# A scaled copy moved to VectorE, activation tables visited together, and a norm's scale and bias folded into weights, in a selective-scan and MLP kernel

## The chip, the cores and the metric

The kernel runs on one core of a Trainium2 chip. A core has five engines that work side by side, each through its own queue in order: TensorE (PE, with its weight loads as PEld), VectorE (DVE), ScalarE (ACT), GpSimd (POOL) and SyncE (SP), which issues most DMAs. Times are microseconds on the device. The median of three runs counts.

## The reference, cut to what matters

The input x has four images of 256 x 64 positions with 128 channels. Layer 0 turns each image into 64 sequences of 256 tokens, runs a selective scan over each in both directions, and adds an MLP:

```python
h = layernorm(xs, g1, b1)
xc, z = split(h @ W_in.T)                       # 2 x 256 channels
# for each direction:
u  = silu(causal_conv(xc))                      # 256 channels, 4 taps
xdbl = u @ Wx_.T                                # 8 + 16 + 16
dt = softplus(xdbl[..., :8] @ Wdt_.T + bdt_)
h_t = exp(dt_t * A) * h_{t-1} + (dt_t * u_t) * B_t   # 16 states a channel
y_t = sum_n h_t[n] * C_t[n];  y = (y + u * D) * silu(z)
# both directions added:
y  = layernorm((y_f + y_b) @ W_out.T, g2, b2)
xo = y + xs
h2 = layernorm(xo, g3, b3)
out = xo + gelu(h2 @ W1m + b1m) @ W2m + b2m
```

A group norm over the whole image stands ahead of layer 0 and of layer 1. Layer 1 projects each position, convolves two 16-channel maps with 3 x 7 kernels and mixes them with products per position ("mixing" below).

## The kernel before

An image is cut into 32 groups of two sequences (512 tokens, `COLS`); with four images there are 128 groups, `G` = 0 to 127. A group has 32 units, one for each direction `i` and state `n`. The main loop runs over the 4096 units `k`, and around each unit it steps generators that hold the rest of the work, one yield or so a step.

For a unit:

- `inputs(k + 3)` makes `dbt`, the product of `duT` (dt times u, tokens on partitions) with one column of B, as four copies of 128x256 scaled by a column, on ScalarE (L472); and `decay`, two exponentials on ScalarE (L478), behind a small GpSimd memset (L476).
- `turned` transposes `dbt` into the PSUM banks `db` on TensorE (L492).
- `scanned` runs two scans on VectorE (L504), one for each half of the channels, with `decay` from SBUF and `db` from PSUM.
- `weighted` multiplies the states by C on GpSimd (L510), in SBUF.
- `added` adds them up over n in PSUM on TensorE (L532); a group's first `added` puts the D term in first (L519).

`dbt`, `decay` and `hs` have four buffers each. The scaled copies run three units ahead of the scans (`AHEAD`), the additions two behind (`LAG`).

For a group, `front(G)` prepares it: load, first norm, convolution on TensorE (L359), silu, the projections (L378, L408), softplus (L307), du on GpSimd (L418), its transposes (L431), then z. It starts `LEAD` units ahead of the group's first one. While it prepares u and dt it is stepped twice a unit. PSUM results are moved out by `evacuated`: on VectorE in the first image (`G < NGRP`, L301 and L303), on ScalarE later (L299). `back(G)` finishes a group: copies of y (L549), gating with z (L561), the output projection, second norm, residual (L571, L574), third norm (L578, L582, L586), MLP up (L591, L593), gelu (L313), MLP down and residual (L615), statistics and store.

`inverse_std` gives a norm's factor: Square on ScalarE (L275), a mean by matmul (L278), then Ln and Exp on ScalarE (L281, L283). A `lock` lets one norm at a time through. Three PSUM banks (`take`, `give`) are shared by fronts, backs, statistics and layer 1; a step that needs one waits until one is free.

ScalarE holds one activation table at a time. Exp and Ln share one, to which `both_tables` (L204) returns after each visit to another: silu (L289, L291), softplus (L307), gelu (L313). `softplus` also runs the gelu of any back that stands in `waiting`; a back that was not taken along within three steps runs its own. Within an engine, the framework orders instructions by program order and its own estimate of when each is ready; `keep_in_program_order` pins an instruction behind all that was written before it on its engine.

In the first image layer 1 has no work yet. From the second on, `project` and `mix` run beside the scans, with large VectorE products and sums (L755, L840, L851, L766); when all units are done, `mix_alone` does the rest.

Of the kernel before, what the change touches and what calls it, by code (L numbers as in the profile page):

```python
# [13 lines left out]
F32 = mybir.dt.float32  # L14
AF = mybir.ActivationFunctionType
ALU = mybir.AluOpType
AX = mybir.AxisListType
PSUM = bass.MemoryType.PSUM
# [14 lines left out]
COLS = 512  # L33
# [6 lines left out]
def fused_kernel(ctx: ExitStack, tc: tile.TileContext, a: dict, out: bass.AP):  # L40
    nc = tc.nc
    x = a["x"]
    B, T, N, _ = x.shape
    SG = COLS // T
    NGRP = N // SG
    TH = T // 128
    RB = 128 // N
    CB = COLS // 128
# [4 lines left out]
    KVT = (T + 2) * N  # L53
    AHEAD, LAG = 3, 2
    UNITS = 2 * NS
    LEAD = 50


    const = ctx.enter_context(tc.tile_pool(name="const", bufs=1))
# [14 lines left out]
    centre = const.tile([128, 128], F32, name="centre")  # L74
# [17 lines left out]
    g1, b1, g2, b2, g3, b3 = (column(f"L0_conv_{k}") for k in ("g1", "b1", "g2", "b2", "g3", "b3"))  # L92
    b1m, b2m = column("L0_conv_b1m"), column("L0_conv_b2m")
# [6 lines left out]
    w1m = load("w1m", [128, FF], a["L0_conv_W1m"])  # L100
# [25 lines left out]
    nc.vector.tensor_scalar(w_om, w_om, 1.0 / C, None, ALU.mult)  # L126
    for h in range(2):
        nc.vector.tensor_scalar(w_out[:, h, :], w_out[:, h, :], w_om[:, h, :], None, ALU.subtract)


    w_cv, neg_a, diag_d = [], [], []
# [30 lines left out]
    p1 = ctx.enter_context(tc.tile_pool(name="p1", bufs=1))  # L162
# [36 lines left out]
    def later(turns):  # L199
        for _ in range(turns):  # L200
            yield 1, 0
# [65 lines left out]
    waiting = []  # L267
    pending = []

    def inverse_std(centred):  # L270
        while lock:
            yield 1, 0
        lock.append(1)
        sq = p1.tile([128, COLS], F32, name="sq")
        nc.scalar.activation(sq, centred, AF.Square)  # L275
        yield 1, 1
        var = take()
        nc.tensor.matmul(var, lhsT=mean_c, rhs=sq, start=True, stop=True)  # L278
        yield 1, 0
        rstd = p1.tile([128, COLS], F32, name="rstd")  # L280
        nc.scalar.activation(rstd, var, AF.Ln, bias=eps_ln)  # L281
        give(var)
        nc.scalar.activation(rstd, rstd, AF.Exp, scale=-0.5)  # L283
        yield from later(2)
        return rstd

    def silu(*ts):
# [15 lines left out]
            nc.vector.tensor_scalar(to, bank, bias, None, ALU.add)  # L303

    def softplus(*ts):
        for dt in ts:
            nc.scalar.activation(dt, dt, AF.Softplus)  # L307
        gelu()
        both_tables()

# [6 lines left out]
    def front(G):  # L317
# [15 lines left out]
        xg = st["xg"] = p3.tile([128, COLS], F32, name="xg")  # L333
# [6 lines left out]
        rstd = yield from inverse_std(xc)  # L340
# [13 lines left out]
        for q in range(4):  # L354
            i, h = divmod(q, 2)
            cv = take()
            for k in range(KC):
# [3 lines left out]
                    lhsT=w_cv[i][:, k, h * 128 : (h + 1) * 128],  # L361
                    rhs=hp[:, :, o : o + T],
                    start=k == 0,
                    stop=k == KC - 1,
# [27 lines left out]
        bT = st["bT"] = p2.tile([128, 2, CB, NS], F32, name="bT")  # L392
# [12 lines left out]
        for q in range(4):  # L405
            i, h = divmod(q, 2)
            v = take()
            nc.tensor.matmul(v, lhsT=w_dt[i][:, h * 128 : (h + 1) * 128], rhs=xds[i], start=True, stop=True)  # L408
            yield 1, 0
            evacuated(G, dts[i][:, h, :], v, bdt[i][:, h : h + 1])  # L410
            give(v)
            yield (0, 1) if q < 3 else (1, 0)
        softplus(*dts)
        yield from later(2)
        for i in range(2):
# [8 lines left out]
            duT = st["duT", i] = p2.tile([128, CB, DI], F32, name="duT")  # L424
# [19 lines left out]
        for h in range(2):  # L444
# [3 lines left out]
                lhsT=w_z[:, h * 128 : (h + 1) * 128],  # L448
                rhs=h_in,
                start=True,  # L450
                stop=True,
# [14 lines left out]
    def inputs(G, i, n):  # L466

        st = state[G]
        dt, bT, duT = st["dt", i], st["bT"], st["duT", i]
        dbt = st["dbt", i, n] = p4.tile([128, CB, DI], F32, name="dbt")  # L470
        for j in range(CB):
            nc.scalar.mul(dbt[:, j, :], duT[:, j, :], bT[:, i, j, n : n + 1])  # L472
        da = st["da", i, n] = p4.tile([128, 2 * SG, T], F32, name="decay")
        lo = 1 - i

        nc.gpsimd.memset(da[:, :, (T - 1) * i : (T - 1) * i + 1], 0.0)  # L476
        for h in range(2):
            nc.scalar.activation(  # L478
                da[:, h * SG : (h + 1) * SG, lo : lo + T - 1],
                dt[:, h, :].rearrange("d (s t) -> d s t", s=SG)[:, :, lo : lo + T - 1],  # L480
                AF.Exp,
                scale=neg_a[i][:, h, n : n + 1],
            )
        if n == NS - 1:
            st[("half", "read")[i]] = True
# [56 lines left out]
    def back(G):  # L542

        b, g = divmod(G, NGRP)
        st = state[G]
        xg, sz = st["xg"], st["s"]
        yt = p1.tile([128, CB, 2, 128], F32, name="yt")
        for k in range(2):
            nc.scalar.copy(yt[:, 2 * k : 2 * k + 2], y[k])  # L549
        while (G > 0 and not state[G - 1].get("back")) or "silu" not in st:  # L550
            yield 1, 0
        xin = p1.tile([128, TH, SG, C], F32, name="xin2")
        nc.sync.dma_start(out=xin, in_=x_cols(b, g))
        yield 1, 1
        yz = p1.tile([128, 2, COLS], F32, name="yz", tag="wide")
        for h in range(2):
            yc = take()
            for j in range(CB):
                nc.tensor.transpose(yc[:, 128 * j : 128 * (j + 1)], yt[:, j, h, :], ident)
            yield 1, 0  # L560
            nc.vector.tensor_tensor(yz[:, h, :], yc, sz[:, h, :], ALU.mult)  # L561
            give(yc)
            yield (0, 1) if h == 0 else (1, 1)
        st["gated"] = True
        oc = take()
        for h in range(2):
            nc.tensor.matmul(oc, lhsT=w_out[:, h, :], rhs=yz[:, h, :], start=h == 0, stop=h == 1)
        yield 1, 0
        rstd = yield from inverse_std(oc)
        xo = p1.tile([128, COLS], F32, name="xo")  # L570
        nc.vector.scalar_tensor_tensor(xo, oc, g2, rstd, ALU.mult, ALU.mult)  # L571
        lock.pop()
        give(oc)
        nc.vector.scalar_tensor_tensor(xo, xo, b2, xg, ALU.add, ALU.add)  # L574
        st["joined"] = True
        yield 1, 1
        xc3 = take()
        nc.tensor.matmul(xc3, lhsT=centre, rhs=xo, start=True, stop=True)  # L578
        yield 1, 0
        rstd = yield from inverse_std(xc3)  # L580
        h3 = p1.tile([128, COLS], F32, name="h3")
        nc.vector.scalar_tensor_tensor(h3, xc3, g3, rstd, ALU.mult, ALU.mult)  # L582
        lock.pop()
        give(xc3)
        yield 1, 0
        nc.scalar.activation(h3, h3, AF.Identity, bias=b3)  # L586
        yield 1, 1
        ge = p1.tile([128, 2, COLS], F32, name="ge", tag="wide")
        for h in range(2):
            m1 = take()  # L590
            nc.tensor.matmul(m1, lhsT=w1m[:, h * 128 : (h + 1) * 128], rhs=h3, start=True, stop=True)  # L591
            yield 1, 0
            nc.vector.tensor_scalar(ge[:, h, :], m1, b1m[:, h : h + 1], None, ALU.add)  # L593
            give(m1)
            yield (0, 1) if h == 0 else (1, 0)
        st["ge"] = ge
        waiting.append(st)
        for _ in range(3):
            if "gelu" not in st:
                yield 1, 0  # L600
        if "gelu" not in st:
            gelu()
            both_tables()
        yield from later(2)
        yield 1, 1

        m2 = take()
        for h in range(2):
            nc.tensor.matmul(
                m2, lhsT=w2m[:, h, :], rhs=ge[:, h, :], start=h == 0, stop=False, skip_group_check=True  # L610
            )
        turned_x(m2, xin, add=True)
        yield 1, 0
        x1 = p1.tile([128, COLS], F32, name="x1")
        nc.vector.scalar_tensor_tensor(x1, m2, b2m, xo, ALU.add, ALU.add)  # L615
        give(m2)
        yield 1, 1
        nc.vector.bn_stats(im[b]["stats2"][:, g, :], x1)
        op = take()
        for j in range(CB):  # L620
            nc.tensor.transpose(op[:, 128 * j : 128 * (j + 1)], x1[:, 128 * j : 128 * (j + 1)], ident)
        yield 1, 0
        ot = p1.tile([128, SG, TH, C], F32, name="ot")
        nc.scalar.copy(ot.rearrange("t s h c -> t (s h c)"), op)
        give(op)
        yield 1, 0
        for h in range(TH):
            nc.sync.dma_start(
                out=im[b]["x1d"][128 * h : 128 * (h + 1), g * SG : (g + 1) * SG, :], in_=ot[:, :, h, :]
            )  # L630
        st["back"] = True
        if g == NGRP - 1:
            yield 1, 0
            yield from group_norm(im[b]["stats2"], im[b]["gn2"])
# [358 lines left out]
    for k in range(len(units) + LAG):  # L993
        G, at = divmod(k, UNITS)
# [119 lines left out]
```

## Time and profile before

| | us |
|---|---|
| median of 3 runs | 19500.96 (19493.19 to 19508.58) |
| profiled execution | 19461.56 (span 19459.8) |
| busy PE, PEld | 16942.8 (87%), 13087.9 (67%) |
| busy DVE | 16298.0 (84%) |
| busy ACT | 16155.3 (83%) |
| busy POOL | 11335.3 (58%) |

The costliest groups of the page are the GpSimd multiply L510 (4096 of 2375 ns), the scans L504 (8192 of 1203 ns), the scaled copies L472 (16384 of 499 ns, overlapping by some 75 ns) and the exponentials L478 (8192 of 711 ns). There are 995 table loads of 1283 ns: 420 at L204, 195 at L307, 128 each at L289 and L313, 124 elsewhere. Busy shares over the whole span mix stages that differ, so the stages are to be read apart.

### The profile page before, as it was taken

The numbers are of one execution on the slowest core, as the hardware profiler recorded it, in microseconds if no ns is written. First come the engines' busy times: TensorE is split into PE (matmuls) and PEld (weight loads), VectorE is DVE, ScalarE is ACT, GpSimd is POOL, SyncE is SP. The second block draws the span as 40 slices with busy tenths as digits, with TensorE's granted clock in tenths as the row PEclk, the third lists the DMA queues.
The fourth block names the chain that finished last, engine by engine and source line by source line (L and its number), as shares of the span: only waits on it lengthen the run. The fifth ranks groups of instructions, "written<-read, shape, count | busy, mean of one in ns | idle before, by whom it ended". The sixth has DMA issues, their size and how long they took to land. (4 is left out here: it accounts for less than half of the span.)

```text
span 19459.8 us, 310011 instructions
## 1 busy us (share of the span) xinstructions
PE 16942.8 (87%) x109608; PEld 13087.9 (67%) x109608; DVE 16298.0 (84%) x13626; ACT 16155.3 (83%) x31245; POOL 11335.3 (58%) x9001
## 2 busy tenths in 40 slices
PE   6999988888888888888888888888888888888788
PEld 4666666666666666666666666666666666666677
DVE  5877777768898888888888888888888888888788
ACT  6999999998887888888888888888888888888322
POOL 4777666665555555555555555555555555555454
PEclk9999999999999999999999999999999999999899
DMA  2232222222332222222232222322222222232222
GB/s 76 86 87 86 80 79 79 79 81 78 90 87 75 80 85 81 80 83 89 84 82 83 81 78 79 87 80 79 81 84 80 80 86 79 81 86 78 68 72 66
DMA packets 1321091, 1574.85 MB, mean 81 GB/s; under 512 B 343232, under 2 KB 704880, under 8 KB 1319536
## 3 DMA queue, kind: packets, MB, share of 16 engines
q1 hardware_dynamic: 1318000, 1554.40, 27.7%
q8 instruction: 865, 14.17, 0.3%
q14 instruction: 690, 5.65, 0.1%
q10 hardware_dynamic: 1536, 0.63, 0.0%
HBM read 1420.15 MB, written 134.45 MB: 80 GB/s over the span
## 5 line engine op out<-in xcount | busy, mean ns | idle before, releaser
L510 POOL TENSOR_TENSOR hs<-hs,cc 128x1024 f32<-128x1024 f32 x4096 | 9717.3, 2375 | 6891.3 <-issue 3003.3
L504 DVE TENSOR_TENSOR_SCAN hs<-decay,db 128x512 f32<-128x512 f32 x8192 | 9503.4, 1203 | 1262.4 <-PE db L492 844.8
L472 ACT ACTIVATE dbt<-duT,bT 128x256 f32<-128x256 f32 x16384 | 7051.8, 499 | 470.6 <-PE db L492 467.3
L478 ACT ACTIVATE decay<-dt,neg_a 128x510 f32<-128x510 f32 x8192 | 5443.3, 711 | 764.3 <-DVE hs L504 755.1
L492 PE MATMUL db<-ident,dbt 128*128 128x128 f32 x32768 | 4999.5, 284 | 1017.7 <-DVE hs L504 890.8
L492 PEld LDWEIGHTS db<-ident,dbt 128*128 128x128 f32 x32768 | 3860.4, 145 | 2710.4 <-DVE hs L504 1403.8
L532 PE MATMUL y<-ident,hs 128*128 128x128 f32 x32768 | 4453.2, 280 | 2.4 <-POOL hs L510 2.4
L532 PEld LDWEIGHTS y<-ident,hs 128*128 128x128 f32 x32768 | 3868.9, 145 | 156.9 <-issue 140.2
L359 PE MATMUL mm<-hpad,w_cv 128*128 128x512 f32 x4096 | 1937.8, 597 | 37.7 <-ACT hpad L348 14.1
L755 DVE TENSOR_TENSOR pr<-qkv,mm 128x2048 f32<-128x2048 f32 x374 | 852.6, 2280 | 544.0 <-PE mm L750 245.0
L359 PEld LDWEIGHTS mm<-hpad,w_cv 128*128 128x128 f32 x4096 | 702.9, 190 | 592.3 <-issue 521.9
L755 DVE TENSOR_TENSOR pr<-mm,ker 128x2048 f32<-128x2048 f32 x421 | 955.3, 2269 | 4.3 <-ACT ker L932 2.4
L766 DVE TENSOR_TENSOR pr<-mm,nv 128x2048 f32<-128x2048 f32 x374 | 849.3, 2271 | 20.3 <-PE mm L750 17.8
L851 DVE TENSOR_REDUCE nv<-pr 128x128 f32<-128x2048 f32 x376 | 852.3, 2267 | 1.0
L840 DVE TENSOR_REDUCE ker<-pr 128x128 f32<-128x2048 f32 x376 | 851.2, 2264 | 0.3
L777 PE MATMUL mm<-ident,pr 128*128 128x128 f32 x5936 | 751.9, 280 | 82.6 <-DVE pr L766 74.9
L777 PEld LDWEIGHTS mm<-ident,pr 128*128 128x128 f32 x5936 | 683.3, 144 | 208.6 <-DVE pr L766 101.4
L418 POOL TENSOR_TENSOR du<-dt,u 128x1024 f32<-128x1024 f32 x256 | 617.6, 2412 | 301.2 <-ACT dt L307 217.8
L766 POOL TENSOR_TENSOR decay<-qkv,duT 128x1024 f32<-128x1024 f32 x272 | 544.6, 2028 | 385.4 <-ACT duT L920 288.3
L431 PE MATMUL mm<-ident,du 128*128 128x128 f32 x2048 | 383.0, 305 | 334.9 <-POOL decay L476 243.5
L204 ACT ACT_TABLE_LOAD x420 | 538.9, 1283 | 5.6
L519 PEld LDWEIGHTS y<-diag_d,u 128*128 128x128 f32 x4096 | 491.7, 198 | 51.2 <-ACT yt L549 25.3
(284 smaller groups left out, 19239.0 us busy)
## 6 DMA issues: line engine op xcount, KB each, us to landing
cc<-cd SPq DMA_DIRECT2D x4096, 256.0 KB
cols<-kv_img SPq DMA_DIRECT2D x444, 210.0 KB
xin<-in_x SPq DMA_DIRECT2D x256, 256.0 KB
kv_img<-kv_pad SPq DMA_DIRECT2D x896, 64.0 KB
cols<-kv_img SPq DMA_DIRECT2D x222, 252.0 KB
xst<-in_x SPq DMA_DIRECT2D x128, 256.0 KB
x1d<-ot SPq DMA_DIRECT2D x256, 128.0 KB
xt<-x1d SPq DMA_DIRECT2D x128, 256.0 KB
```

The lines of the kernel that those rows point to most:

```text
L359: nc.tensor.matmul(cv.rearrange("c (s t) -> c s t", s=SG), lhsT=w_cv[i][:, k, h * 128 : (h + 1) * 128], rhs=hp[:, :, o : o + T], start=k == 0,
L472: nc.scalar.mul(dbt[:, j, :], duT[:, j, :], bT[:, i, j, n : n + 1])
L478: nc.scalar.activation(da[:, h * SG : (h + 1) * SG, lo : lo + T - 1], dt[:, h, :].rearrange("d (s t) -> d s t", s=SG)[:, :, lo : lo + T - ...
L492: last = nc.tensor.transpose(db[:, 128 * j : 128 * (j + 1)], dbt[:, j, 128 * h : 128 * (h + 1)], ident)
L504: nc.vector.tensor_tensor_scan(dh, d0, d1, 0.0, ALU.mult, ALU.add)
L510: nc.gpsimd.tensor_tensor(hs, hs, cc[:, None, :].to_broadcast([128, 2, COLS]), ALU.mult)
L532: nc.tensor.matmul(y[j // 2][:, j % 2, h, :], lhsT=hs[:, h, 128 * j : 128 * (j + 1)], rhs=ident, is_transpose=True, start=False, stop=i == ...
L755: nc.vector.tensor_tensor(pr, left.rearrange("p (a e) -> p a e", e=16)[:, :, None, :].to_broadcast([128, na, nb, 16]), right.rearrange("p ...
L766: eng.tensor_tensor(pr.rearrange("p e (a b) -> p e a b", b=nb), left[:, :, :, None].to_broadcast([128, n, na, nb]), right[:, :, None, :].t ...
L777: nc.tensor.matmul(to, lhsT=p, rhs=ident, is_transpose=True, start=k == 0, stop=stop and k == len(blocks) - 1, skip_group_check=True,)
L840: nc.vector.tensor_reduce(ker.rearrange("p (n d) -> p n d", d=DD), pr, AX.X, ALU.add)
L851: nc.vector.tensor_reduce(nv.rearrange("p (v n) -> p v n", n=NH), pr, AX.X, ALU.add)
```

## The change

- In the first image, the last of a unit's four scaled copies is done by VectorE.
- `softplus` takes its two tiles in reversed order, each pinned in program order, so that both and the gelu of a waiting back stand together; ahead of it a front waits up to five steps while no back is waiting.
- The third norm's scale g3 is multiplied into the MLP's weights w1m at the start and its bias b3 goes into the MLP's bias (`b1m_3`). The second norm's bias b2 is left out of xo and taken into account where xo is used: `b2c` (b2 centred) in the third norm, `b2_b2m` at the last residual. The residual addition L574 becomes a GpSimd addition of two SBUF tiles, and the ScalarE pass L586 goes.
- `inverse_std` yields once instead of twice behind the Exp, the step around L586 goes, `LEAD` is 46 instead of 50, and x1 is written over xo.

```diff
-    LEAD = 50
+    LEAD = 46
...
+    b2_b2m = const.tile([128, 1], F32, name="b2_b2m")
+    nc.vector.tensor_tensor(b2_b2m, b2, b2m, ALU.add)
+    b2c = const.tile([128, 1], F32, name="b2c")
+    b1m_3 = const.tile([128, 2], F32, name="b1m_3")
+    with tc.tile_pool(name="prep_ps", bufs=1, space=PSUM) as prep_ps:
+        m = prep_ps.tile([128, 4], F32, name="m")
+        nc.tensor.matmul(m[:, 0:1], lhsT=centre, rhs=b2, start=True, stop=True)
+        for h in range(2):
+            nc.tensor.matmul(m[:, 1 + h : 2 + h], lhsT=w1m[:, h * 128 : (h + 1) * 128], rhs=b3, start=True, stop=True)
+        nc.vector.tensor_copy(b2c, m[:, 0:1])
+        nc.vector.tensor_tensor(b1m_3, m[:, 1:3], b1m, ALU.add)
+    nc.vector.tensor_scalar(w1m, w1m, g3, None, ALU.mult)
...
-    def inverse_std(centred):
+    def inverse_std(centred, bias=None):
...
-        nc.scalar.activation(sq, centred, AF.Square)
+        nc.scalar.activation(sq, centred, AF.Square, **({} if bias is None else {"bias": bias}))
...
-        yield from later(2)
+        yield 1, 0
         return rstd
...
     def softplus(*ts):
-        for dt in ts:
-            nc.scalar.activation(dt, dt, AF.Softplus)
+        for dt in reversed(ts):
+            tc.keep_in_program_order(nc.scalar.activation(dt, dt, AF.Softplus))
         gelu()
         both_tables()
...
+        for _ in range(5):
+            if G > 2 and not waiting:
+                yield 1, 0
         softplus(*dts)
...
         for j in range(CB):
-            nc.scalar.mul(dbt[:, j, :], duT[:, j, :], bT[:, i, j, n : n + 1])
+            if G < NGRP and j == CB - 1:
+                nc.vector.tensor_scalar(dbt[:, j, :], duT[:, j, :], bT[:, i, j, n : n + 1], None, ALU.mult)
+            else:
+                nc.scalar.mul(dbt[:, j, :], duT[:, j, :], bT[:, i, j, n : n + 1])
...
-        nc.vector.scalar_tensor_tensor(xo, xo, b2, xg, ALU.add, ALU.add)
+        nc.gpsimd.tensor_tensor(xo, xo, xg, ALU.add)
...
-        rstd = yield from inverse_std(xc3)
+        rstd = yield from inverse_std(xc3, b2c)
         h3 = p1.tile([128, COLS], F32, name="h3")
-        nc.vector.scalar_tensor_tensor(h3, xc3, g3, rstd, ALU.mult, ALU.mult)
+        nc.vector.scalar_tensor_tensor(h3, xc3, b2c, rstd, ALU.add, ALU.mult)
         lock.pop()
         give(xc3)
-        yield 1, 0
-        nc.scalar.activation(h3, h3, AF.Identity, bias=b3)
         yield 1, 1
...
-            nc.vector.tensor_scalar(ge[:, h, :], m1, b1m[:, h : h + 1], None, ALU.add)
+            nc.vector.tensor_scalar(ge[:, h, :], m1, b1m_3[:, h : h + 1], None, ALU.add)
...
-        x1 = p1.tile([128, COLS], F32, name="x1")
-        nc.vector.scalar_tensor_tensor(x1, m2, b2m, xo, ALU.add, ALU.add)
+        x1 = xo
+        nc.vector.scalar_tensor_tensor(x1, m2, b2_b2m, xo, ALU.add, ALU.add)
```

## The prediction

> **What bounds the kernel now.** I read the busy time of each engine by stage first, then the waits of ScalarE and VectorE, then the groups of instructions, then single stretches of the timeline. Following the scans along the timeline (2048 for each image), the first scan of the four images starts at 198.8, 3935.7, 8613.8 and 13371.8 us, and the last scan ends at 18084.8. So the first image takes 3737 us for its 1024 units, the next three 14149 us for 3072 units, and 1375 us of mixing follow. Two inner stretches stand for the first image and for the other three (columns: stretch, length, then busy us and instructions of PE, PEld, DVE, ACT, POOL):
>
> ```profile
> 1000.00:3900.00 2900.00, 2628.67 (x16430) 1926.61 (x16428) 2232.93 (x2264) 2795.19 (x5416) 2011.75 (x1629) 0.97 0.28 81
> 5000.00:17900.00 12900.00, 11250.61 (x72835) 8690.57 (x72834) 11269.53 (x9046) 11058.78 (x21219) 7341.07 (x5923) 0.96 0.29 82
> ```
>
> In the first image ScalarE is busy 2795 of 2900 us (96%) and VectorE only 77%: ScalarE bounds it. The stretch holds 1579 scans, 789.5 units, so a unit takes 3.67 us: ScalarE 3.54, VectorE 2.83, GpSimd 2.55. In the later images (5572 scans, 2786 units, 4.63 us each) VectorE has 4.05, TensorE 4.04 and ScalarE 3.97 us a unit: three engines at 86 to 87%, none of them the bound alone.
>
> The waits in the first stretch show what a second bound would meet:
>
> ```profile
> ACT dbt L472 <- PE db L492: 32.1, 33, 1.8
> DVE u L303 <- PE y L519: 109.4, 23, 7.0
> DVE duT L301 <- PE mm L431: 86.2, 28, 6.0
> ```
>
> ScalarE hardly waits. VectorE waits 109 + 86 us for TensorE results that stand in queue order ahead of its scans; with the waits of L454 (33.6) and L615 (35.9) these are 265 us, 0.33 us a unit, and a faster ScalarE doesn't remove them all.
>
> [...]The trace agrees on the lock, both ways (start, length, engine, line):
>
> ```profile
> 8156.26 2.83 DVE L574 SCALAR_TENSOR_TENSOR xo<-xo,L_conv_b,xg 128x512 f32<-128x512 f32 x1
> ...
> 8156.17 2.38 POOL L510 TENSOR_TENSOR hs<-hs,cc 128x1024 f32<-128x1024 f32 x1
> 8158.47 2.83 POOL L418 TENSOR_TENSOR du<-dt,u 128x1024 f32<-128x1024 f32 x1
> ```
> ```profile
> 1.51 0.67 DVE L75 TENSOR_SCALAR centre<-ident 128x128 f32<-128x128 f32 x1 [0.28 <-POOL ident masks.py:199]
> ...
> 1.43 0.52 POOL L79 TENSOR_SCALAR_AFFINE_SELECT group_c<-group_c 128x128 f32<-128x128 f32 x1
> ```
>
> L574 has two SBUF inputs: it began 0.09 us after GpSimd's multiply and ended 0.55 us after it; then the GpSimd multiply behind it took 2.83 us where the median is 2.36. L75 is a tensor_scalar, as the new copy is: 0.67 us beside GpSimd, ending 0.23 us after GpSimd was done. [...]the trace has 1283 ns for every load.
>
> **The change, part by part.**
>
> ```profile
> L574 DVE SCALAR_TENSOR_TENSOR xo<-xo,L_conv_b,xg 128x512 f32<-128x512 f32 x25 | 18.5, 741 | 0.5
> L586 ACT ACTIVATE h<-h,L_conv_b 128x512 f32<-128x512 f32 x25 | 17.7, 708 | 0.0
> ```
> ```profile
> L574 DVE SCALAR_TENSOR_TENSOR xo<-xo,L_conv_b,xg 128x512 f32<-128x512 f32 x87 | 182.3, 2095 | 2.3
> L204 ACT ACT_TABLE_LOAD x261 | 334.9, 1283 | 2.9
> L307 ACT ACT_TABLE_LOAD x152 | 195.0, 1283 | 2.7
> L313 ACT ACT_TABLE_LOAD x87 | 111.6, 1283 | 1.6
> L478 ACT ACT_TABLE_LOAD x50 | 64.2, 1283 | 0.9
> L586 ACT ACTIVATE h<-h,L_conv_b 128x512 f32<-128x512 f32 x87 | 62.3, 716 | 0.2 <-DVE h L582 0.2
> ```
>
> (The first two lines are of the first image's stretch, 25 groups; the other six of the later one, 87 groups.)
>
> *Copies, first image.* Four copies follow each other in 1.70 us on ScalarE, 0.425 each; one fewer in 1024 units is 435 us less. On VectorE each adds one 128x256 tensor_scalar with a column as scalar. The nearest row is L151, 128x128 of the same kind: 283 ns, 203 ns from start to start. [...]0.35 us long, 0.27 us of VectorE's queue. To this comes the wait for the lock, which no row shows. I bound it by laying all scan ends of units 64 to 999 beside the GpSimd multiply then running: right behind a unit's second scan GpSimd is on average 0.16 us from its next boundary (it starts on that scan's result 0.13 us later, so the copy mostly wins); behind any other VectorE instruction it is 1.18 us. The copy's buffer is one of four and free early, so I expect it behind the second scan mostly; 407 of 936 second scans are followed by a scan, the rest by an evacuation that can stand ahead of the copy. I take four in five well placed: 0.8 x 0.16 + 0.2 x 1.18 = 0.36 us; ends 0.16 and 0.74 (43% well placed).
>
> *Table visits.* The pinned softplus pair saves the 65 loads that 152 has over 87 and as many returns (the 50 at L478 among them); a gelu behind softplus saves one return for each of 87 groups. That is up to 217 loads in 87 groups, 3.2 us a group, 0.10 us a unit of ScalarE. In the first image pairs are together already (25 loads for 25 groups), so only the 24 returns go: 31 us of 2900, 0.039 a unit. The front waits up to five steps, 2.5 units; behind it GpSimd's du and the transposes wait, which the next group's units need, by my count of the front's steps, some nine units later. I cost that at nothing, and at 3.7 us a unit if the cover is gone.
>
> *Third norm.* L586 goes: 0.022 us a unit of ScalarE. L574 leaves VectorE: 0.023 us a unit in the first image, 182.3/2786 = 0.065 in the later ones, because it waits for the lock there. GpSimd gets an add of half the size of its 2.37 us multiply, estimated 1.2 us a group, 0.04 a unit, at 57% busy: hidden; what waits for it is the centring matmul, 33 times after L574 now. The bias in Square adds under 0.1 us a group, three matmuls and a few column operations at the start under 3 us beside the loads. Fewer steps per norm and LEAD 46 move work without adding any: between -50 and +50 us, taken as nothing. One tile fewer costs nothing: the backs are serial already.
>
> **Sum.** First image: ScalarE 3.54 - 0.425 - 0.022 - 0.039 = 3.05 us a unit; VectorE 2.83 + 0.27 - 0.02 + 0.36 = 3.44, and half of its 0.33 us of waits for TensorE on top, 3.60. VectorE becomes the bound: 0.07 x 1024 = **70 us less**, where ScalarE alone would promise over 400. Later images: VectorE -0.065, ScalarE -0.12, TensorE unchanged. Following VectorE alone this is 200 us of 3072 units, following ScalarE 370, following TensorE nothing; I take 0.045, **140 us**. The profiled execution took 19461.56 us (span 19459.8), 39 us under the median 19500.96. Minus 210 it is 19252, set against the median about 19290; I say **19300**.
>
> **The rivals.**
> 1. [...]With the copy behind evacuations as often as half the time the wait is 0.74 us, the VectorE unit 3.98, the first image 320 us longer; minus 140 this is +180: 19680. For it: 57% of second scans are followed by something else, and 1.18 us each. Against: the copy is ready units ahead. The total turns slower from a mean wait of about 0.57 us.
> 2. *Softplus and gelu don't meet.* Around 2098 softplus runs some ten units ahead of the gelu at 2141; the wait covers 2.5, three dropped steps and the banks freed meanwhile must give the rest. Then 128 returns stay, 164 us of ScalarE: about 100 us faster in all, 19400.
> 3. *TensorE holds the later images* (4.04 of 4.63 us) and VectorE the first: within noise, 19500.
> 4. *Everything pays.* Lock wait 0.16 (first image -270), later images after ScalarE and VectorE (-230): 19000.
>
> **How the numbers follow.** My forecast 0.40; rivals 0.23, 0.17, 0.10, 0.10. About 0.2%, 39 us, can be told from no change. Faster: 0.40, 0.14 of rival 2, 0.10 of rival 4 and 0.02 of rival 3, **0.66**; within it 0.09; slower 0.25. The range, 19050 to 19640, leaves out the outer ends of rivals 1 and 4; the forecast's own is 19180 to 19420.
>
> **What would show it.** First image: ScalarE well under 96% busy, VectorE the busiest; the new copy at the multiply's old line with minimum near 0.35 us and a mean between 0.5 and 1.1; GpSimd's multiply above 2375 ns on average; a unit near 3.6 us. Later images: L574's line on GpSimd, about 1.2 us; 128 softplus loads, gelu loads right behind them, some 220 to 290 fewer loads than 995 in all; 4.57 us a unit. I am wrong if the copy shows no lock wait (first image near 3.4), if its mean is over 0.9 us, or if the later images don't move.

## The result and the profile after

The changed kernel took **20104.39 us** (median of 3, 20091.15 to 20127.54) against 19500.96: ratio **1.0318** [1.0304, 1.0332]. It is slower, well outside the range of the prediction. The profiled span is 20102.7 us, 643 longer. Following the scans, the first image took 4081.4 us (+344), images 2 to 4 together 14467.0 against 14149.0 (+318), the mixing at the end 28 less, and the first scan began 8 later.

The two inner stretches of the changed kernel (stretch, length, then busy us and instructions of PE, PEld, DVE, ACT, POOL):

```profile
1000.00:3900.00 2900.00, 2461.51 (x15081) 1822.79 (x15080) 2558.12 (x2789) 2268.06 (x4193) 1882.12 (x1520) 0.95 0.27 75
5000.00:18500.00 13500.00, 11597.97 (x74432) 8967.38 (x74431) 11367.14 (x9154) 11056.07 (x21409) 7574.60 (x6137) 0.95 0.29 80
```

In the first stretch ScalarE fell from 96% to 78% and VectorE rose from 77% to 88%, as forecast, but the stretch holds 726 units where it held 789.5: 3.99 us a unit. The second stretch holds 2846 units, 4.74 us each (before 4.63). There VectorE has 3.99 us a unit (before 4.05) and ScalarE 3.88 (before 3.97): **both do less per unit, and the unit takes longer**. TensorE alone has slightly more, 4.08 (before 4.04).

The groups of instructions of the first stretch have the copies as one row (behind the bar: busy us, mean ns, idle us ahead), and the timeline shows two of them (start, length, engine, line):

```profile
L493 DVE TENSOR_SCALAR dbt<-duT,bT 128x256 f32<-128x256 f32 x723 | 590.5, 821 | 0.0
```
```profile
1999.79 2.42 POOL L533 TENSOR_TENSOR hs<-hs,cc 128x1024 f32<-128x1024 f32 x1
...
2002.14 0.32 DVE L493 TENSOR_SCALAR dbt<-duT,bT 128x256 f32<-128x256 f32 x1
...
2016.00 2.37 POOL L533 TENSOR_TENSOR hs<-hs,cc 128x1024 f32<-128x1024 f32 x1 [1.53 <-ACT dbt L495]
2016.90 1.66 DVE L493 TENSOR_SCALAR dbt<-duT,bT 128x256 f32<-128x256 f32 x1
...
2018.49 1.20 DVE L527 TENSOR_TENSOR_SCAN hs<-decay,db 128x512 f32<-128x512 f32 x1
```

The copy at 2002.14 came as a multiply was ending and took 0.32 us. The one at 2016.90 began 0.90 us into a multiply, ended 0.19 us after it, and took five times as long; the next scan came behind it. Of all 1024 copies 413 began while GpSimd stood idle and took 0.33 us on average; the other 611 took 1.15 and ended 0.19 us (median) after GpSimd's instruction. This wait is all that "lock" stands for here; why the one engine waits for the other is not shown. VectorE alone paid here: GpSimd's multiply, at 2370 ns on average in this stretch with a copy waiting beside it or not, was no longer than before (2374).

The waits of the first stretch, answering to those of before:

```profile
ACT decay L501 <- DVE hs L527: 312.4, 244, 6.2
ACT dbt L495 <- PE db L515: 138.0, 87, 5.8
DVE hs L527 <- PE db L515: 124.9, 92, 3.2
DVE duT L315 <- PE mm L450: 87.9, 23, 3.9
```

ScalarE's copies waited 32 us for TensorE's transposes before and 138 now, and its exponentials 312 us for scans, where it was 12.5. VectorE's wait for `duT` stands as it was (86 to 88). The two scans of a unit, which stood idle for 311 us of the stretch before, still do for 180:

```profile
L504 DVE TENSOR_TENSOR_SCAN hs<-decay,db 128x512 f32<-128x512 f32 x1579 | 1832.8, 1205 | 311.4 <-PE db L492 195.5 <-ACT decay L478 40.7 <-ACT dbt L472 40.5
```
```profile
L527 DVE TENSOR_TENSOR_SCAN hs<-decay,db 128x512 f32<-128x512 f32 x1452 | 1690.7, 1200 | 180.5 <-PE db L515 124.9 <-issue 35.9 <-ACT rstd L295 19.3
```

Of the later images these groups answer to those shown of before (89 groups of two sequences; before 87):

```profile
L218 ACT ACT_TABLE_LOAD x227 | 291.2, 1283 | 3.7
L614 DVE TENSOR_SCALAR ge<-mm,b1m 128x512 f32<-128x512 f32 x178 | 131.3, 738 | 138.6 <-PE mm L612 138.3
L322 ACT ACT_TABLE_LOAD x91 | 116.8, 1283 | 1.6
L328 ACT ACT_TABLE_LOAD x89 | 114.2, 1283 | 1.5
L597 POOL TENSOR_TENSOR xo<-xo,xg 128x512 f32<-128x512 f32 x89 | 113.5, 1276 | 99.8 <-DVE xo L594 99.8
```

The loads fell as far as the low end of the forecast: softplus 152 to 91, returns 261 to 227, 775 in the whole run where there were 995. The addition on GpSimd takes 1276 ns (estimated 1.2 us). New is the idle time at L614, the MLP's bias: 138.6 us of VectorE standing for a matmul; before it was

```profile
L593 DVE TENSOR_SCALAR ge<-mm,L_conv_b1m 128x512 f32<-128x512 f32 x174 | 127.3, 733 | 2.8 <-PE mm L591 2.3
```

### The profile page after: what moved, and what is told of

Same layout as the page of the kernel before. It is cut to its first block, busy times and chain, and to the rows that moved or that the text cites. A ratio compares the mean times of both kernels' runs of the same rounds, so it can differ in the third digit from the quotient of the medians.

```text
span 20102.7 us, 308966 instructions
## 1 busy us (share of the span) xinstructions
PE 17106.6 (85%) x109614; PEld 13252.6 (66%) x109614; DVE 16837.8 (84%) x14526; ACT 15482.4 (77%) x29873; POOL 11464.7 (57%) x9129
## 5 line engine op out<-in xcount | busy, mean ns | idle before, releaser
L533 POOL TENSOR_TENSOR hs<-hs,cc 128x1024 f32<-128x1024 f32 x4096 | 9698.3, 2370 | 7315.6 <-issue 3550.9
L495 ACT ACTIVATE dbt<-duT,bT 128x256 f32<-128x256 f32 x15360 | 6625.5, 499 | 576.3 <-PE db L515 570.1
L555 PE MATMUL y<-ident,hs 128*128 128x128 f32 x32768 | 4517.4, 281 | 38.0 <-POOL hs L533 37.5
L555 PEld LDWEIGHTS y<-ident,hs 128*128 128x128 f32 x32768 | 3909.3, 146 | 212.4 <-issue 166.8
L798 PE MATMUL mm<-ident,pr 128*128 128x128 f32 x5968 | 808.6, 291 | 149.4 <-DVE pr L787 143.0
L798 PEld LDWEIGHTS mm<-ident,pr 128*128 128x128 f32 x5968 | 731.6, 151 | 258.2 <-DVE pr L787 146.0
L493 DVE TENSOR_SCALAR dbt<-duT,bT 128x256 f32<-128x256 f32 x1024 | 834.9, 820 | 0.0
L450 PEld LDWEIGHTS mm<-ident,du 128*128 128x128 f32 x2048 | 282.0, 162 | 399.8 <-POOL decay L499 189.6
```

Of the source, the lines that this page charges most:

```text
L533: nc.gpsimd.tensor_tensor(hs, hs, cc[:, None, :].to_broadcast([128, 2, COLS]), ALU.mult)
L555: nc.tensor.matmul(y[j // 2][:, j % 2, h, :], lhsT=hs[:, h, 128 * j : 128 * (j + 1)], rhs=ident, is_transpose=True, start=False, stop=i == ...
L798: nc.tensor.matmul(to, lhsT=p, rhs=ident, is_transpose=True, start=k == 0, stop=stop and k == len(blocks) - 1, skip_group_check=True,)
```

## The experiments

A step, or turn, is one `yield` of a generator. The fold is the third norm's part of the change, the pair the two pinned softplus, and the wait the up to five steps ahead of them. In the expectations, A is the theory that the lock, the copy's wait for GpSimd, makes the first image slower, B that shortened sequences of steps make all four images wait, C that the single turn behind the Exp makes the later ones slow, D that fold and table visits hinder each other. All times are set against runs of the kernel before on the same chip (medians 19476 to 19487; 19501 for the whole change). The last two columns are from the traces: from the first scan of the first image to that of the second, and from there to the end of the last scan. Each is from one execution. The executions of one kernel lie 10 to 50 us apart, so differences below that say little.

| run | edit | ratio (95%) | first image | images 2 to 4 |
|---|---|---|---|---|
| before | | 1 | 3736.9 | 14149.0 |
| after | the whole change | 1.0318 [1.0304, 1.0332] | 4081.4 | 14467.0 |
| c1 | before + copies | 1.0195 [1.018, 1.021] | 4118.5 | 14146.0 |
| c2 | after without copies | 1.0146 [1.0129, 1.0163] | 3751.8 | 14471.0 |
| c7 | before + pinned copies | 1.0042 [1.0025, 1.0059] | 3834.7 | 14142.3 |
| c8 | before + copies that also sum | 1.0014 [1.0007, 1.0021] | 3765.2 | 14165.6 |
| c9 | before, fourth copy left out | 0.9905 [0.989, 0.9919] | 3557.3 | 14165.0 |
| c3 | before + fold | 1.0039 [1.0024, 1.0054] | 3685.2 | 14323.3 |
| c10 | before + fold, step kept | 0.9995 [0.9986, 1.0004] | 3704.6 | 14185.5 |
| c6 | before + one turn behind the Exp | 1.0085 [1.007, 1.01] | 3718.4 | 14380.3 |
| c12 | before + LEAD 46 | 0.9937 [0.992, 0.9954] | 3736.4 | 14036.4 |
| d1 | before + LEAD 48 | 0.9995 [0.9986, 1.0003] | 3756.1 | 14146.7 |
| d5 | before + pinned softplus | 0.9900 [0.9885, 0.9915] | 3726.2 | 13979.7 |
| d4 | d5 + wait | 1.0007 [0.9998, 1.0016] | 3765.1 | 14151.5 |
| c4 | d4 + LEAD 46 | 0.9918 [0.9903, 0.9933] | 3739.2 | 14000.3 |
| e1 | c10 + pinned softplus | 0.9914 [0.9897, 0.993] | 3703.1 | 14030.8 |
| e2 | e1 + LEAD 46 | **0.9866 [0.9852, 0.9881]** | 3697.5 | 13954.4 |
| c15 | e2 + wait | 1.0022 [1.0014, 1.003] | 3735.9 | 14216.4 |
| c5 | c15, step dropped | 1.0088 [1.0073, 1.0103] | 3761.8 | 14356.5 |
| d3 | c2 with LEAD 50 | 1.0149 [1.0134, 1.0164] | 3864.8 | 14357.5 |

### Which part makes which image slower

c1 is the kernel before with the hunk of the copies alone, c2 the changed kernel without it.

```diff
+            if G < NGRP and j == CB - 1:
+                nc.vector.tensor_scalar(dbt[:, j, :], duT[:, j, :], bT[:, i, j, n : n + 1], None, ALU.mult)
+            else:
                 nc.scalar.mul(dbt[:, j, :], duT[:, j, :], bT[:, i, j, n : n + 1])
```

> The kernel before with one edit: in the first image the last of four scaled copies of a unit on VectorE. Theory A [...]: the first image takes 300 to 400 us longer (4081 us in the changed kernel against 3737), the later images stay within 40 us, total about 19850 us; the copy's mean is 0.75 to 0.9 us where its minimum is 0.32. Theory B (the shortened steps and the new waits make the queues stall in all four images, the copy is cheap): at most 100 us longer, about 19550 us.

> The changed kernel with all four scaled copies back on ScalarE. Theory A: the first image returns to about 3700 us, the later ones keep their 318 us excess, total about 19750 us. Theory B: the first image stays near 4000 us, total about 20000 us.

The loss splits by image. The copies alone make the first image 382 us longer (330 on top of the rest of the change) and leave the others as they were; without them the first image is at 3752 and the others as slow as in the changed kernel (14471 and 14467). So there are two causes. The mean of all copies in c1 was 0.93 us, a little more than A allowed.

### The first image: lock, relief, or queues

c7 pins the VectorE copy directly behind the second scan of a unit. c8 leaves it unpinned and uses the form that also writes out its sum. That this form doesn't wait for GpSimd was an assumption of the author that no trace had shown; c8 bears it out: all 1024 copies took 448 to 482 ns, though 711 began beside a GpSimd instruction. c9 leaves the fourth copy out, so that its first image lacks the factor B for a quarter of the tokens.

```diff
# c7, in the main loop
             scanned(k)
+            if k + AHEAD < len(units):
+                copied(*units[k + AHEAD])     # the VectorE copy, in keep_in_program_order
             weighted(k)
# c8
-                nc.vector.tensor_scalar(..., None, ALU.mult)
+                nc.vector.tensor_scalar(..., None, ALU.mult, ALU.add, accum_out=unused)
# c9, in inputs and in turned
+            if G < NGRP and j == CB - 1:
+                continue
...
+            src = state[G]["duT", i] if G < NGRP and j == CB - 1 else dbt
...
```

> The kernel before with the copies on VectorE in the first image, each pinned behind the unit's second scan. Theory A [...]: more of the copies stand behind a second scan, their mean falls from 0.82 us to 0.35 to 0.5, the first image from 4118 us to 3450 to 3750, total 19200 to 19500 us. If the added VectorE work itself is the cost, whatever its place: the first image stays above 3950 us.

> The kernel before with the copies on VectorE in the first image, unpinned, in the form that also writes the sum over the row (to a column that nothing reads). Theory A[...]: the copy's mean is close to its minimum, about 0.5 to 0.6 us with the write of the sum, longer than 0.32 but without the tail; the first image 3500 to 3800 us, total about 19300 to 19550 us. If the tail comes from something else: mean above 0.8 us, total above 19800 us.

> The kernel before with the fourth scaled copy left out in the first image: TensorE transposes that quarter straight from duT, so that the scaling by B of a quarter of the tokens is missing from the first image, and neither ScalarE nor VectorE does the copy. It prices the relief of ScalarE without any cost elsewhere. If ScalarE's 96% was the bound (the prediction's step), ScalarE needs about 3.10 us a unit, VectorE 2.83, and the first image falls from 3737 us to 3200 to 3350. If in-order waits between TensorE's transposes, the scans and the exponentials hold the period anyway, ScalarE falls to about 85% busy and the first image stays at 3600 to 3740 us. Images 2 to 4 unchanged (4678, 4758, 4713) within 10 us.

The groups of instructions in c7 (1000 to 3700 us), c8 and c1 (1000 to 3900 us):

```profile
L497 DVE TENSOR_SCALAR dbt<-duT,bT 128x256 f32<-128x256 f32 x722 | 389.0, 539 | 0.0
```
```profile
L475 DVE TENSOR_SCALAR_CACHE_REDUCE dbt<-duT,bT 128x256 f32<-128x256 f32 x787 | 361.4, 459 | 2.5
L475 DVE DVE_READ_ACCUMULATOR dbt<-duT,bT 128x1 f32 x787 | 65.4, 83 | 0.0
```
```profile
L474 DVE TENSOR_SCALAR dbt<-duT,bT 128x256 f32<-128x256 f32 x718 | 672.2, 943 | 0.0
```

In c1 a copy takes 943 ns on average; pinned it takes 539 (of units 64 to 999, 834 stand behind the second scan at 352 ns, 102 elsewhere at 2156), and the first image loses 98 us in place of 382. With the sum it takes 459 + 83 ns and never waits, and the first image loses 28. In c8 VectorE has the same copies to do and each is longer than a copy without a wait, so the lock is the cause of most of the loss: A holds. c7 fell between its two expectations, 85 us above what A allowed it. And the form that never waits brings no gain either. c9 helps to tell why, in its stretch of the first image:

```profile
1000.00:3700.00 2700.00, 2500.36 (x16116) 1887.12 (x16115) 2183.68 (x2225) 2445.13 (x4535) 1974.30 (x1599) 0.98 0.28 86
```

With no engine doing the copy the first image gains 180 us, not the 435 that ScalarE is spared; this too lies between the two expectations. TensorE is then the busiest, 2500 of 2700 us (93%), ScalarE second (91%); TensorE had 2629 of 2900 us (91%) before, in the very line that showed ScalarE's 96%. In c8 no engine is above 89% and a unit still takes 3.68 us: from 1000 to 3900 us the scans stand 178 us for transposes, ScalarE's exponentials 135 us for scans.

### The later images: work or steps

First each part alone. c3 is the fold, with the step that stood ahead of L586 dropped as in the change; c10 keeps that step. c6 has one turn behind the Exp.

```diff
# c3 (with b2c, b2_b2m, b1m_3 as in the change)
-        nc.vector.scalar_tensor_tensor(xo, xo, b2, xg, ALU.add, ALU.add)
+        nc.gpsimd.tensor_tensor(xo, xo, xg, ALU.add)
...
-        yield 1, 0                                     # stays in c10
-        nc.scalar.activation(h3, h3, AF.Identity, bias=b3)
# c6
-        yield from later(2)
+        yield 1, 0
         return rstd
```

> The kernel before with the third norm's scale and bias folded, the residual addition on GpSimd, the ScalarE pass gone, x1 written over xo; LEAD 50, two turns behind the Exp and softplus as before. By the forecast's own sum (VectorE 0.065 us a unit less in the later images, ScalarE 0.02): 100 to 200 us faster, about 19350 us. If the GpSimd addition delays the back and what queues behind it, the later images' excess is here: about 19700 us.

> The kernel before with the third norm folded into the weights (as in the run of the fold alone, ratio 1.0039), but the step that stood ahead of the left-out ScalarE pass kept, so that the back has as many steps as before. If the shortened sequence of steps made the fold slower (images 2 to 4 together 75 us longer), this run is at or below the kernel before: 19350 to 19490. If the addition on GpSimd or the tile shared by xo and x1 makes it slower, it stays near 19555.

> The kernel before with one turn instead of two behind the Exp of inverse_std. Theory C: 200 to 370 us slower, 19700 to 19850 us, in the later images, with VectorE and ScalarE waiting for each other at the norms (rows of hn, xo, h and hpad). Theory D: within 60 us of before.

The fold adds 174 us to images 2 to 4 with the step dropped and 37 with the step kept: that step is 138 us, though it holds no instruction. One turn less is 231 us, and no instruction differs but table loads, of which there are fewer (724 to 659 in these images). c6's whole time, 168 us longer, falls short of the 200 that C asked for, and of the waits that C named the one at `hpad` doesn't appear. c3's time lies between its two expectations, c10's where the shortened sequence of steps put it. What the fold itself does here is small: 32 us less in the first image, nothing in the second and third (+2, -1), 36 more in the fourth, although VectorE is 0.06 us a unit less busy.

c12 and d1 change LEAD alone; d5 pins the softplus pair, d4 adds the wait, c4 adds LEAD 46.

```diff
# c12 (d1: 48)
-    LEAD = 50
+    LEAD = 46
# d5
-        for dt in ts:
-            nc.scalar.activation(dt, dt, AF.Softplus)
+        for dt in reversed(ts):
+            tc.keep_in_program_order(nc.scalar.activation(dt, dt, AF.Softplus))
# d4 and c4, ahead of softplus
+        for _ in range(5):
+            if G > 2 and not waiting:
+                yield 1, 0
```

> The kernel before with LEAD 46 instead of 50 and nothing else: no instruction added or removed. If the work of each engine decides, it takes the same 19480 within 0.2%. If the position of the steps of fronts, backs and mixing against the units decides the later images, they move by 0.5 to 1.5% to either side although the counts of all instructions but table loads stay equal; the first image stays at 3737 within 30 us.

> The kernel before with LEAD 48 and nothing else. If an earlier start of the fronts costs steadily (banks and queue places held longer), the later images are about half as much shorter as with LEAD 46: 55 us, 19420. If the position of the steps picks one of several patterns without such an order, it lies anywhere from 19300 to 19650; outside 19380 to 19450 speaks for that.

> The kernel before with the two softplus in reversed order and pinned, nothing else: no wait, LEAD 50. It has the step count of the kernel before, so it prices the saved table loads alone. The prediction's step (152 softplus loads against 87 groups, as many returns) gives about 60 loads of 1.28 us less in images 2 to 4, some 100 us of ScalarE, and if half of that reaches the period: 19400 to 19450. If table loads are not on the path of the later images, 19480 within 0.2%.

> The kernel before with the pinned softplus and the wait of up to five steps, LEAD left at 50. LEAD 46 alone gave 0.9937, pin, wait and LEAD 46 together 0.9918. If the table visits are worth something by themselves, this is at 0.993 to 0.997. If nearly all came from LEAD, it is at 0.998 to 1.002.

> The kernel before with the softplus pair pinned and reversed, the wait of up to five steps ahead of it and LEAD 46; two turns behind the Exp and the norm as before. If the later images' excess comes from the longer single absence of ScalarE and the held front: about 19750 us. If table visits only save loads: 50 to 150 us faster, about 19400 us.

LEAD 46 gives 113 us, 109 of them in the second image; LEAD 48 gives 2. So the answer to LEAD isn't steady, and d1 lies outside the band that a steady one was given. Part of the 113 us may be table loads: c12 has 44 fewer, 56 us of ScalarE. c4, with pair, wait and LEAD 46, is 163 us faster, a little more than its expectation allowed.

The pinned pair alone, with every step where it was, has 578 loads in images 2 to 4 where there were 724: 146 x 1.283 = 187 us of ScalarE, and the images are **169 us shorter**. That is more than the expectation allowed. It is no steady price of a load, though: each of the three images has 44 to 54 loads fewer, and they gain 71, 98 and 0 us. Groups 84 to 93 have their four mixing blocks at the same distances in both runs; there two loads less a group (2.6 us) make it 6.5 us shorter (146.8 to 140.2). In groups 108 to 123 1.6 loads less make it no shorter (146.9 and 147.5). On top of the fold (e1 against c10, below) the same saving gives 52, 61 and 42 us.

The wait of five steps then takes all of it away (13979.7 to 14151.5); d4 stands where "nearly all came from LEAD" put it, but not for that reason. 31 of the loads come back in d4, 40 of the 172 us at most if each counts in full. Its second image is the slowest second image of these runs, in a pattern that repeats from group to group. The stretches of that pattern in d4, and of the one that d5 settles into (the last three figures are the granted clock of TensorE, the DMA share and GB/s):

```profile
5600.00:7800.00 2200.00, 1887.65 (x11981) 1448.46 (x11980) 1843.85 (x1487) 1793.13 (x3463) 1200.58 (x973) 0.94 0.27 79
```
```profile
7300.00:8300.00 1000.00, 901.42 (x5974) 699.42 (x5972) 917.88 (x740) 886.33 (x1731) 603.79 (x488) 0.98 0.29 86
```

and their groups of instructions, d4 first (behind the bar: busy us, mean ns, then the idle time ahead and what ended it):

```profile
L509 DVE TENSOR_TENSOR_SCAN hs<-decay,db 128x512 f32<-128x512 f32 x915 | 1067.6, 1204 | 201.2 <-PE db L497 161.1 <-ACT dt L299 19.6 <-ACT decay L483 19.1
L483 ACT ACTIVATE decay<-dt,neg_a 128x510 f32<-128x510 f32 x915 | 611.9, 713 | 195.6 <-DVE hs L509 195.3
```
```profile
L505 DVE TENSOR_TENSOR_SCAN hs<-decay,db 128x512 f32<-128x512 f32 x460 | 531.2, 1202 | 13.7 <-PE db L493 12.5 <-POOL hs L511 1.0 <-ACT dbt L473 0.3
L479 ACT ACTIVATE decay<-dt,neg_a 128x510 f32<-128x510 f32 x458 | 303.1, 708 | 27.3 <-DVE hs L505 27.3
```

Two scans are a unit: d4 has 457.5 units, 4.81 us each, d5 230 at 4.35. VectorE's work is 4.03 and 3.99 us of it, nearly equal. What differs is that the scans stand idle for 0.44 us a unit in d4, mostly for transposes, and for 0.06 in d5, and the exponentials 0.43 for scans against 0.12. A group then takes 153.6 us or 140.1.

TensorE's time isn't equal: 4.13 and 3.92 us a unit, at a granted clock of 0.94 and 0.98. The trace of d4 shows the clock at half 44 times in that stretch, 242 us in all (d5: 10 times, 48 us). In the 3.4 us ahead of each (as long as the shortest stretches at half clock in the traces of before and after), TensorE had been busy for 47% (median); over equal pieces at full clock it was 97%. So the half clock came behind waits of TensorE; that the waits bring it about is not shown. A transpose in it takes 427 ns where it takes 277 at full clock, and follows the one before it after 213 ns instead of 109. How much of the slow pattern comes with the half clock, and what starts it, no run separates.

Last, the whole change step by step. e1 is c10 with the pinned pair, e2 has LEAD 46 as well; c15 adds the wait to e2, c5 drops the step ahead of L586, c2 drops the turn. d3 is c2 with LEAD 50.

```diff
# c15 to c5
         give(xc3)
-        yield 1, 0
         yield 1, 1
```

> The kernel before with the two parts that leave the steps in place: the fold with its step kept (0.9995 alone) and the pinned softplus pair without wait (0.9900 alone), LEAD 50. If the parts add once no step is moved, images 2 to 4 take about 14149 + 36 - 169 = 14016 us and the run 0.989 to 0.991 (19270 to 19310). If fold and table visits hinder each other by themselves (by the GpSimd addition or the shared tile), it lies at 0.995 or above.

> The same with LEAD 46. With the wait of five steps added, this is the run that took 1.0022 (images 2 to 4 at 14216). If the wait was what cost there, this one is below 0.992 with images 2 to 4 under 14050. If LEAD 46 doesn't fit the folded back, it is at 0.998 or above.

> The changed kernel with the scaled copies on ScalarE and both dropped steps put back (two turns behind the Exp, the step ahead of the left-out pass): fold, pinned softplus, wait and LEAD 46 remain. The same with only the two turns back took 1.0088 of the kernel before, with neither 1.0146. If the dropped steps are what makes fold and visits together slower, this one is near the visits alone: 0.988 to 0.995 (19250 to 19390). If the GpSimd addition and the visits hinder each other, it stays at 1.006 or above.

> The changed kernel with the copies back on ScalarE and two turns behind the Exp of inverse_std again. Folding alone cost 75 us and the visits with LEAD 46 alone gained 163; with one turn all of it together cost 284. Theory C (the single turn makes the later images slow): about 19400 us, the sum of the two. Theory D (folding and visits get in each other's way, the turn is harmless): stays near 19760 us.

> The changed kernel with the scaled copies on ScalarE and LEAD 50 again: same work as the run at 1.0146, fronts started four units earlier. If the position of the steps decides, the later images move by more than 40 us to either side (time outside 19720 to 19810). If fewer steps behind each norm make other engines wait wherever the front stands, it stays at 19760 within 40 us.

From 14149.0, images 2 to 4 go to 13954.4 with fold, pair and LEAD 46, then up: wait **+262**, dropped step **+140**, dropped turn **+115**, copies -4, which is 14467.0. These are prices in this order only. Turn and LEAD cost something else elsewhere (231 and 115; -113 before, -76 from e1 to e2, -151 from d4 to c4, +114 from d3 to c2). The dropped step comes to the same sum beside everything else (140) as in the kernel before (138), but that is chance: by image it is +80, -17, +77 here and +4, +97, +37 there.

c5 and c15 both fell between their two expectations, hence e1 and e2. D falls for fold and pair: once no step is moved they add up (e1: 14030.8 against the expected 14016). With the wait and LEAD 46 the fold isn't small: c15 is c4 with the fold, all steps kept, and images 2 to 4 are 216 us longer than in c4, where fold alone was 37 and beside the pair 51 (e1 against d5). So the prices of fold, wait and LEAD depend on one another, and the +262 is not the wait's alone.

d3's time stands within the band that meant "wherever the front stands", but only because two movements cancel: images 2 to 4 are 114 us shorter than in c2 and the first is 113 longer. From c5 to c2, with the turn dropped, the waits at the MLP's bias (L614) and at `hpad` (L363; lines of the changed kernel) grow from 0.25 and 0.37 us a group to 1.5 and 1.1. In d3 they are 2.5 and 0 and in c6 0.6 and 0, so they aren't what the turn costs everywhere.

e2 is the best version, 19227.14 us against 19486.62 on its chip. It has the fold and the pair, and none of the copies, the wait or the dropped steps.

## Why the prediction was wrong

**First image, forecast -70, measured +344.** The mechanism was named: the copy meets the lock, VectorE becomes the busiest, ScalarE drops (78%). The sum promised 3.60 us a unit and 3.99 came. Two of its terms failed, and so did the hope beside it.

- *Four in five copies well placed.* It was half: of the 938 copies in the time of units 64 to 999, 470 stood behind a second scan (0.36 us each, nearly no wait), but 308 stood between the two scans of a unit (1.12), which was not considered, and 160 elsewhere (1.61). The length without the wait was 0.32 us (the least; 0.33 on average), where 0.35 had been taken: L151's 283 ns and the author's addition for the greater width, which no trace had shown. The mean of all was 0.82, so the wait was 0.50 us where 0.36 was taken. VectorE came to 3.515 us a unit over the whole first image, forecast 3.44.
- *Waits of the scans, taken at nothing.* This is the larger miss. "Half of its 0.33 us of waits for TensorE" was right: the four waits counted in it, 265 us of the stretch, came down to 102 (`duT` 87.9, u 13.5, the others under 1), 0.14 us a unit. But the sum had no term for the scans' own waits, 311 us before, 0.39 a unit. 180 of them stayed (0.25), and 0.08 stayed elsewhere. Together VectorE stood idle for 0.47 us a unit in the changed kernel, 0.45 in c7 and 0.48 in c8, where 0.16 was taken. 3.515 + 0.47 is the 3.99 measured.
- *ScalarE alone would promise over 400.* c9 shows 180. TensorE's work, 3.31 us of a unit's 3.65 over the first image, left some 0.33 us to gain, 340 us in all, before any wait was counted; the line that the prediction quoted had it at 91%. This is no hard limit, as TensorE's own time fell to 3.22 us in c9, and what stopped c9 at half of it is not shown.

Rival 1, by which the copy's wait decides, had the mechanism, and nearly the size (+320 for the first image) by luck: its split was wrong, a wait of 0.74 us and little idle time. The turning point of 0.57 us was too high: at 0.50 the first image alone had lost 344. Rival 4's -270 was out of reach even with the copy left out.

GpSimd's multiply was expected above 2375 ns; it stayed at 2370. It was the copy that waited.

**Later images, forecast -140, measured +318.** Some of the savings were there, and the moved steps cost more.

- *Table visits*: the pinned pair was right in size, 130 loads in 87 groups forecast, 146 in 96 measured in d5, and undervalued: d5 gains 169 us for 187 us of loads, e1 155 beside the fold, unevenly from image to image. A load takes 1283 ns, and the trace shows hardly any idle time around it: ScalarE stands 18 ns ahead of a load and 11 ns behind it (medians of 994 in the kernel before). The gelu behind softplus, 87 returns forecast, is rival 2's point, and there the rival was right: with the wait but both turns (d4, c4, c15, c5) the returns stay at 419 in the whole run, as many as without it (420). There the wait bought no visit. Only with the single turn as well do they fall, to 345 in the changed kernel; with the single turn and no wait (c6) they stay at 419.
- *Third norm* was taken as 0.065 us of VectorE a unit, part of it on the path. VectorE was spared this much in c10, and images 2 to 4 gained nothing. Of L574's 96 executions there before, 80 began beside a GpSimd instruction and took 2.33 us, the other 16 took 0.73: most of what was saved was waiting. In the changed kernel Square takes 676 ns with the bias and 584 in the other norms, and the matmuls and column operations at the start 2.4 us, as estimated.
- *"Fewer steps per norm and LEAD 46 move work without adding any: between -50 and +50, taken as nothing."* This is the step that failed. Measured: LEAD between -151 and +114, the dropped step about +140, the dropped turn +115 to +231.
- *The wait, costed at nothing* because the next group needs its inputs some nine units later. It cost 172 us in d4 and 262 in c15. In d4's second image softplus is still done ten units ahead of the group's first scan, so the cover held and the cost was not lateness. That it comes from moving what stands behind it in the queues is the likely reading, but isn't shown; 31 and 37 table loads came back with it (at most 40 and 47 us).

**What stays open.** The runs show that moved steps select a repeating pattern of 140 to 158 us a group with nearly the same instructions, and what a slow pattern looks like: scans behind transposes, exponentials behind scans, TensorE's clock lower. They don't show what makes a position good. In d4, in c6 and d3 at the end, and in the slowest stretch of the changed kernel (groups 84 to 93, 157.5 us), the widest gap between two of a group's four mixing blocks is 17 units, and in e2's 141 us pattern 13; but c4 and c15 have the same gaps (5, 6, 15, 6) in groups 108 to 123 and take 143.7 and 149.3. So no rule follows.

## What to carry to other kernels

Before moving work off the busiest engine, read the second busiest in the same stretch (here 91% beside 96%): it bounds what can be hoped for. Then price every wait of the engine that is to become the bound, those of its main instructions too. When an edit takes work out of a hand-stepped schedule, keep the steps where they were and measure any moved step as an edit of its own; here empty steps were worth more than the work. A price found for one edit needn't hold beside another: the fold cost 37 us alone and 216 with the wait and LEAD 46. When a VectorE instruction begun beside a GpSimd one ends only behind it, as these copies did, and isn't pinned, suppose that it meets one about as often as GpSimd is busy: here 60% of the copies, at 65% busy.

## What the runs showed of the hardware that was not expected

A 128x256 fp32 tensor_scalar took 328 ns on average when it began while GpSimd stood idle (413 of 1024); begun beside a GpSimd instruction (611) it ended 0.19 us after it (median) and took up to 2540 ns in all; GpSimd's multiply, on an engine busy 65% of the time, was not longer for it (2370 ns). The same operation with its sum written out took 459 ns and 83 ns for the read of the sum, and in 1024 cases, 711 of them beside a running GpSimd instruction, none took more than 482 ns. Less VectorE time (0.06 us a unit in c10) bought nothing where VectorE was 87% busy, while fewer table loads on ScalarE, busy 86%, gave 155 to 169 us for 187. TensorE's granted clock was at half behind stretches of waiting, in the kernel before too: 259 times from 300 to 18000 us, 1406 us in all, TensorE busy for 33% (median) of the 3.4 us ahead of each, where it was 99% over equal pieces at full clock; transposes took 425 ns in it instead of 277.
